# New prices and transfer rules in the planner that orders a fused feed-forward kernel

## The chip, the cores and the metric

The kernel runs on one core of a Trainium2 chip. Each core has a matrix engine (TensorE, PE in the profile), a vector engine (VectorE, DVE), a scalar engine (ScalarE, ACT), a general engine (GpSimd, POOL) and SyncE (SP), which only issues transfers. Each engine works through its own list of instructions in order; they wait for one another by semaphores. Transfers are issued by an engine's queue and carried out by 16 DMA engines. The metric is the time on the device in microseconds (us).

## The reference

Inputs are x (4 batches x 1024 tokens x 512), a condition (4 x 128) and three weights: norm_w (512 x 128), up_w (4096 x 512) and down_w (512 x 2048). In float32:

```python
scale = cond @ norm_w.T + 1.0
ms = jnp.mean(x * x, axis=-1, keepdims=True)
h = x * (scale[:, None, :] * jax.lax.rsqrt(ms + EPS))
u = h @ up_w.T
val, gate = jnp.split(u, 2, axis=-1)
h = val * jax.nn.gelu(gate, approximate=False)
hq = act_quant(h)      # 8 bits, a scale for each token
wq = weight_quant(down_w)   # -1, 0 or 1, one scale: the mean of |down_w|
return hq @ wq.T + x
```

## The kernel before

**What is computed where.** The up-projection is done with 16-bit floats in high and low parts, so that one product of float32 matrices becomes six matmuls. The first of the four batches is multiplied plainly, in 16 pieces of weights by two halves of 512 tokens (`plain_half`, products by L897, the product of the two halves of the projection by VectorE at L925). While it runs, the weights of each piece are prepared for the later batches: loaded from DRAM (`w_load`, L581), their largest magnitude taken (`w_largest`, L589) and from it a power of two and gain factors (L467, L595 to L604), turned on TensorE (`w_turn`, L625), split into high and low (L639 to L661), summed for a scheme of fast matrix multiplication (L673 to L689), and spilled to a DRAM scratch (`s_spill`, L693). The down weights are loaded (L740), summed (L744) to the mean (L753 to L755) and rounded (L759, L760). Batches two to four use the fast scheme: seven products of half size for each pair of pieces (`product`, L882; copies and combinations L960 to L999), with weight forms reloaded from scratch. The rows of h are then quantised (L1011 to L1086) and multiplied by the down weights in 8-bit floats (L1102, L1153), scaled and added to x (L1111, L1193), and stored.

**The condition.** The scale of each channel is worked out early on VectorE (`scT`, L510, L514) in a layout with channels on partitions. Batches 1 to 3 need it in rows instead: `cond_rows` (L551) writes each column of `scT` to `rows_dram`, 128 x 4 values of four bytes at scattered places, one transfer for each batch, `cond_load_scale` (L556) reads one back, repeated on all partitions, into `sc` (256 KB), and `cond_bring` (L560, VectorE) scales it, for the tokens of the next batch (L829).

```python
SP.dma_start(out=rows_dram[b].rearrange("(k p) -> p k", p=P), in_=scT[:, :, b])   # L551
SP.dma_start(out=sc, in_=rows_dram[b].partition_broadcast(P))                     # L556
DVE.tensor_scalar(sc, sc, ux[:, b : b + 1], None, ALU.mult)                       # L560
```

**The planner.** No engine is called directly. The kernel's functions run against recorders, which note every instruction as a step: its engine, the steps it depends on (by what it reads and overwrites) and its price. `Plan.order` then orders the steps, and `emit` issues them in that order, which is the order of every engine's list. Semaphores are derived from the dependencies afterwards, so that the result of any order is right. The first 150 steps (HEAD) of each engine keep their recorded order. The rest is found in 40 rounds:

- `needed` works out for every step the latest time at which it may start without delaying TensorE, from the times of the round before.
- `place` takes the steps by that latest time and gives each the first free stretch on its engine's line behind its dependencies, with a margin of up to 0, 0.3, 0.6 or 0.9 us, changing from round to round.
- `replay` runs the order through a model of the engines, and sets the prices and times for the next round. Then six replays with chance (each cost but TensorE's times 0.95 to 1.09, each of SyncE's transfers up to 1 us later) give a mean end, and the order with the least mean is taken.

`price` gives for each step its time alone, its time beside work on the port which VectorE and GpSimd share, and for a transfer the time that it keeps the DMA engines. A transfer counts 1.2 us from issue to start and 1.5 us from its last byte to landing. SyncE's transfers share one line, "DMA", one behind the other; ScalarE's don't stand on it. ScalarE issues three transfers: one load in the head, `cond_load_rest` (L488, which brings the condition of batches 1 to 3) and the last store.

Of the kernel before, what the change touches and what calls it, by code (L numbers as in the profile page):

```python
# [78 lines left out]
def _free(v):  # L79
    n = 1  # L80
    for d in v.shape[1:]:
        n *= d
    return n
# [28 lines left out]
class Plan:  # L112
# [12 lines left out]
    def add(self, eng, method, real, args, kwargs):  # L125
# [6 lines left out]
        writes = [a for w, a in operands if w]  # L132
        reads = [a for w, a in operands if not w]
        s.alone, s.beside, s.wait = price(eng, method, writes, reads, args, kwargs)
        deps = set()
        for v in reads:
# [36 lines left out]
        if not s.wait:  # L173
            if s.n < HEAD and eng in self.last:
                deps.add(self.last[eng])
# [5 lines left out]
    def order(self):  # L181

        steps = self.steps
        for s in steps:
            s.after, s.cost = [], (s.alone + s.beside) / 2
        for s in steps:
            for d in s.deps:
                steps[d].after.append(s)
        clock = 0.0
        for s in steps:  # L190
            if s.eng == "PE":
                s.start = clock
                clock += s.cost
        best, chance = None, random.Random(1)
        for n in range(ROUNDS):
            self.needed(clock)
            self.place(0.3 * (n % 4))
            order = sorted(steps, key=lambda s: (s.start, s.n))
            clock = self.replay(order)
            late = sum(self.replay(order, chance) for _ in range(MISSES)) / MISSES  # L200
            if best is None or late < best[0]:
                best = late, order
            self.replay(order)
        self.replay(best[1])
        return best[1]
# [5 lines left out]
            for t in s.after:  # L211
                s.late = min(s.late, t.late - lag(s, t) - s.wait - s.cost)

    def place(self, margin):

        steps = self.steps
        used = {e: Line() for e in ("PE", "ACT", "DVE", "POOL", "SP", "DMA")}
        for s in sorted(steps, key=lambda s: (s.late, s.n)):  # L220
            t = max((steps[d].end + lag(steps[d], s) for d in s.deps), default=0.0)
            if s.eng != "PE":
                t += min(margin, max(0.0, s.late - t) * 0.1)
            if s.wait and s.eng == "SP":
                t = used["DMA"].put(t + ISSUE, s.wait) - ISSUE
            s.start = used[s.eng].put(t - s.before, s.before + s.cost) + s.before
            s.end = s.start + (ISSUE + s.wait + LANDING if s.wait else s.cost)

    def replay(self, order, chance=None):

        steps = self.steps
        free = dict.fromkeys(("PE", "ACT", "DVE", "POOL", "SP", "DMA"), 0.0)
        port = {"DVE": 0.0, "POOL": 0.0}
        for s in order:
            e = s.eng
            t = free[e] + s.before
            for d in s.deps:
                t = max(t, steps[d].end + lag(steps[d], s))
            cost = s.alone
            if s.beside > s.alone:  # L240
                x = port["POOL" if e == "DVE" else "DVE"] - t
                if x > 0:
                    cost += (s.beside - s.alone) * min(1.0, x / s.alone)
                port[e] = t + cost
            if chance:
                cost *= 1.0 if e == "PE" else 0.95 + 0.14 * chance.random()
            else:
                s.cost = (s.cost + cost) / 2 if e in port else cost
            s.start, s.end = t, t + cost
            free[e] = s.end  # L250
            if s.wait and e != "SP":
                s.end = t + ISSUE + s.wait + LANDING
            elif s.wait:
                free["DMA"] = max(free["DMA"], t + ISSUE) + s.wait
                s.end = free["DMA"] + LANDING + (chance.random() if chance else 0.0)
        return max(s.end for s in order)
# [6 lines left out]


HEAD = 150
ROUNDS, MISSES, ISSUE, LANDING, RELOAD = 40, 6, 1.2, 1.5, 6.5


class Line:
# [2 lines left out]
    def __init__(self):  # L272
        self.spans = []

    def put(self, t, cost):
        v = self.spans
        n = bisect.bisect_right(v, (t, 1e9))
        if n and v[n - 1][1] > t:
            t = v[n - 1][1]
        while n < len(v) and v[n][0] < t + cost:  # L280
            t = v[n][1]
            n += 1
        v.insert(n, (t, t + cost))
        return t


def lag(s, t):

    if s.eng == t.eng:
        return 0.0  # L290
    if s.eng == "PE":
        return 0.2
    return 0.08 if t.eng == "POOL" else 0.05


def price(eng, method, writes, reads, args, kwargs):

    out = writes[0]
    n = _free(out)
    if "dma" in method:  # L300
        nbytes = n * out.shape[0] * mybir.dt.size(out.dtype)
        if "transpose" in method:
            return 0.45 + nbytes / 32768 * 0.16, 0.0, nbytes / 32768 * 0.17
        last = min(v.ap[-1][1] * mybir.dt.size(v.dtype) if v.ap[-1][0] == 1 else 4 for v in (out, reads[0]))
        return 0.45, 0.0, nbytes / (290e3 if last >= 1024 else 1.5e3 if last < 64 else 150e3)
    wide = max([n] + [_free(v) for v in reads if len(v.shape) > 1])
    psum = any(str(v.space).endswith("PSUM") for v in reads)
    if eng == "PE":
        f32 = any(v.dtype == F32 for v in reads)
        return (max(n, 64) * (2 if f32 else 1) / 2.4 + 2.5) / 1e3, 0.0, 0.0  # L310
    if eng == "ACT":
        cost = 0.08 + wide * 0.0009 + (0.05 if method != "copy" else 0) + (0.05 if psum else 0)
        return cost, 0.0, 0.0
    if eng == "POOL":
        if method == "partition_all_reduce":
            return (1.8 if wide > 1 else 0.4), 0.0, 0.0
        if method == "tensor_scalar":
            cost = 0.2 + wide * 0.00092
            return cost, cost * 1.2, 0.0
        cost = 0.75 if wide <= 8 else 0.18 + wide * 0.00195  # L320
        return cost, cost * 1.42, 0.0
    if method == "reciprocal":
        return 0.17 + max(0, wide - 8) * 0.0056, 0.0, 0.0
    if wide <= 32:
        return 0.17, 0.0 if psum else 0.44, 0.0
    if psum or method in ("tensor_reduce", "memset"):
        return 0.1 + wide * 0.00108, 0.0, 0.0
    if method == "tensor_scalar":
        cost = 0.1 + wide * 0.00052
        return cost, cost * 2.2, 0.0  # L330
    if method == "tensor_tensor" and all(v.dtype in (BF16, F16) for v in reads):
        cost = 0.1 + wide * 0.00052
        return cost, cost * 1.6, 0.0
    cost = 0.1 + wide * 0.00106
    return cost, cost * (1.35 if method == "scalar_tensor_tensor" else 1.8), 0.0


class Rings:
# [30 lines left out]
def glu_quant_kernel(  # L369
# [557 lines left out]
    def plain_first(between):  # L927

        ps = {1: bank("B", 1, name="pg_0_0"), 0: bank("A", 2, name="pv_0_0")}
        gate, a21, a22 = a_parts(0)  # L930
        order = [(1, w, 0, k) for w in range(2) for k in range(2)]
        order += [(1, w, 0, k) for k in range(2, NK) for w in range(2)]
        order += [(0, w, 0, k) for w in range(2) for k in range(NK)]
        order += [(t, 0, 1, k) for t in (1, 0) for k in range(NK)]
        for n, (t, w, l, k) in enumerate(order):
            if n in between:
                between[n]()
            a = [gate[:, 0], gate[:, 1]] if t else [a21, a22]
            a = a[k // 2].rearrange("p w (k f) -> p w k f", k=2)
            PE.matmul(  # L940
                ps[t], a[:, w, k % 2, :], XP[:, l, k, :TOK],
                start=w + l + k == 0, stop=l == 1 and k == NK - 1,
            )
        t1 = wpool.tile([P, TOK], F32, name="g_0_0", tag="t1")
        ACT.activation(t1, ps[1], AF.Gelu, scale=gain(0, 1))
        DVE.scalar_tensor_tensor(h_half(0, 0), ps[0], gain(0, 0), t1, ALU.mult, ALU.mult)
# [167 lines left out]
    class Pair:  # L1114
# [12 lines left out]
        def sum1(self, place):  # L1127
            self.s[1] = place.bitcast(BF16)
            DVE.tensor_tensor(self.s[1], self.part(1, 0), self.part(1, 1), ALU.add)
# [759 lines left out]
```

## Time and profile before

| | us |
|---|---|
| median of 3 timed runs | 742.27 (742.14 to 743.57) |
| the profiled execution, its own time | 737.92 |
| its span, first to last instruction | 736.1 |

The granted clock of TensorE was 0.998 in the profiled execution. How the page's other numbers are read: an engine's busy time is the time in which it ran instructions that are counted; the rest of the span it waited, or issued. A group or a timeline row gives the line of the kernel, the operation, what it writes and reads, and the shape; x4 means four alike in a row. Of a matmul of 512 columns the duration shown (0.38 us) is longer than the distance between two of them in a row, since they are pipelined. For transfers the row on SPq is only the issue; the time to landing is given apart.

The page's shares by engine in 40 slices show where TensorE is not at 90% or more of the time:

```profile
## 2 busy tenths in 40 slices
PE   6999999999999999999999999999999999999998
DVE  5976899999888767989878988798768888865997
ACT  4876646676245775535344577743333666333373
POOL 1465887789214000714002300750001000000000
DMA  8788678999954444695943445697753444443414
```

Each digit is a slice of 18.4 us. Only the first and the last slices stand under 9. The DMA engines are busiest in slices 4 to 12, which is the first batch, in which weights are loaded and spilled.

### The profile page before, as it was taken

The page shows a single profiled execution, that of the slowest core. Times are in us where ns is not written, and L with a number is a line of the kernel's source. Part 1 is how long each engine was busy: PE and PEld are TensorE (multiplying, and loading weights), DVE is VectorE, ACT ScalarE, POOL GpSimd, SP SyncE. Part 2 cuts the span into 40 slices and gives each one's busy share as a digit, 9 for nine tenths or more (in the row PEclk, how much of TensorE's full clock was granted, in tenths as well). Part 3 has the DMA queues.
Part 4 walks back from the last instruction along what each step waited for, and adds up shares of the span by engine and source line. Part 5 has one row for each costly group of instructions (what it writes and reads, how often), then busy time and mean ns, then how long its engine had stood idle before and what let it go on. Part 6 is the DMA issues. An engine that isn't in the chain of part 4 may idle for free.

```text
span 736.1 us, 10201 instructions
## 1 busy us (share of the span) xinstructions
PE 723.8 (98%) x3684; PEld 363.2 (49%) x3684; DVE 606.6 (82%) x833; ACT 392.1 (53%) x635; POOL 215.5 (29%) x213
## 2 busy tenths in 40 slices
PE   6999999999999999999999999999999999999998
PEld 3554444444444445655444445656444444444754
DVE  5976899999888767989878988798768888865997
ACT  4876646676245775535344577743333666333373
POOL 1465887789214000714002300750001000000000
PEclk9999999999999999999999999999999999999999
DMA  8788678999954444695943445697753444443414
GB/s 267 244 175 206 192 203 210 233 250 236 229 162 101 100 102 137 159 206 154 233 135 101 108 101 140 159 208 155 183 141 106 97 100 108 104 101 97 144 38 164
DMA packets 179567, 115.74 MB, mean 157 GB/s; under 512 B 141750, under 2 KB 147767, under 8 KB 179516
## 3 DMA queue, kind: packets, MB, share of 16 engines
q1 hardware_dynamic: 179226, 114.76, 60.7%
q10 hardware_dynamic: 290, 0.33, 0.3%
q8 instruction: 29, 0.48, 0.3%
q14 instruction: 22, 0.18, 0.1%
HBM read 58.93 MB, written 23.09 MB: 111 GB/s over the span
## 4 chain that ended last, share of the span: by engine, by line
PE 88%; DMA 5%; DVE 3%; ACT 3%; issue 1%; POOL 1%; SPq 0%; POOLq 0%; DVEq 0%
PE A L882 33%; PE E L882 17%; PE B L882 8%; PE po L1153 8%; PE E L897 8%; PE B L897 4%; PE A L897 4%; DMA rows_dram<-scT 2%; PE po L1102 2%; PE E L1102 1%; PE A L1102 1%; DMA s_dram<-R 1%; DMA H<-in_x_dram 1%; DMA am<-in_x_dram 1%; ACT R L1218 1%
## 5 line engine op out<-in xcount | busy, mean ns | idle before, releaser
L882 PEld LDWEIGHTS <-SXY 128*128 128x128 f16 x2016 | 197.2, 98 | 229.8 <-issue 2.1
L882 PE MATMUL A<-R,SXY 128*128 128x512 f16 x1152 | 270.5, 379 | 0.3 <-ACT t L960 0.3
L882 PE MATMUL E<-R,SXY 128*128 128x512 f16 x576 | 142.9, 379 | 0.0
L1032 POOL PARTITION_ALL_REDUCE am<-R x8 | 17.3, 2158 | 249.1 <-DVE R L1018 249.1
L1074 DVE TENSOR_TENSOR H<-H,am 128x1024 f32<-128x1024 f32 x64 | 78.7, 1260 | 0.1
L897 PEld LDWEIGHTS <-SXY 128*128 128x128 f16 x462 | 45.1, 98 | 53.5
L882 PE MATMUL B<-R,SXY 128*128 128x512 f16 x288 | 70.8, 379 | 0.0
L1016 DVE TENSOR_REDUCE gm<-H 128x512 f32<-128x1024 f32 x56 | 68.9, 1230 | 0.7
L980 DVE SCALAR_TENSOR_TENSOR H<-A,sg,t 128x512 f32<-128x512 f32 x48 | 35.9, 748 | 36.0 <-PE A L882 35.7
L968 ACT COPY B<-A 128x512 f32<-128x512 f32 x48 | 27.4, 570 | 60.1 <-PE A L882 56.7
L1153 PE MATMUL po<-wd,R 128*128 128x256 fp8e4 (+1 forms) x448 | 59.0, 275 | 0.0
L993 ACT ACTIVATE t<-t,sg 128x512 f32<-128x512 f32 x48 | 34.7, 722 | 39.2 <-DVE t L990 39.1
L1153 PEld LDWEIGHTS <-R 128*128 128x128 bf16 (+1 forms) x480 | 47.0, 98 | 15.9
L960 ACT COPY t<-A 128x512 f32<-128x512 f32 x48 | 28.1, 586 | 48.9 <-PE A L882 48.8
L990 DVE TENSOR_TENSOR t<-E,t 128x512 f32<-128x512 f32 x48 | 33.0, 688 | 24.4 <-PE E L882 24.0
L977 ACT ACTIVATE t<-B,sg 128x512 f32<-128x512 f32 x48 | 33.0, 687 | 34.5 <-PE B L882 34.0
L786 POOL TENSOR_SCALAR ssq<-ssq 128x2 f32<-128x2 f32 x12 | 5.5, 456 | 155.4 <-ACT H L816 114.1
L897 PE MATMUL E<-R,SXY 128*128 128x512 f16 x210 | 49.6, 379 | 0.0
L996 DVE TENSOR_TENSOR v<-A,v 128x512 f32<-128x512 f32 x48 | 33.1, 689 | 19.7 <-PE A L882 18.0
L972 ACT COPY v<-E 128x512 f32<-128x512 f32 x48 | 28.1, 586 | 34.0 <-PE E L882 31.6
L1018 DVE TENSOR_TENSOR R<-R,gm 128x512 f32<-128x512 f32 x56 | 44.4, 792 | 0.8
L897 PEld LDWEIGHTS <-R 128*128 128x128 f16 x282 | 27.5, 98 | 33.6 <-issue 1.3
(232 smaller groups left out, 1082.0 us busy)
## 6 DMA issues: line engine op xcount, KB each, us to landing
SXY<-s_dram SPq DMA_DIRECT2D x66, 256.0 KB, 2.7
SXY<-s_dram SPq DMA_DIRECT2D x18, 384.0 KB, 3.6
H<-in_L_cond_up_w_dram SPq DMA_DIRECT2D x13, 512.0 KB, 4.9
s_dram<-SXY SPq DMA_DIRECT2D x14, 384.0 KB, 4.9
xr<-in_x_dram SPq DMA_DIRECT2D x19, 256.0 KB, 3.3
out_dram<-xr SPq DMA_DIRECT2D x19, 256.0 KB, 3.6
H<-in_x_dram SPq DMA_DIRECT2D x8, 512.0 KB, 5.5
R<-in_L_cond_down_w_dram SPq DMA_DIRECT2D x8, 512.0 KB, 6.5
```

The costliest lines, as they stand in the source:

```text
L882: PE.matmul(o, s[:, w, k, :], tv[:, :, c, l, k, :], start=start and n == 0, stop=stop and n == len(TERMS) - 1, skip_group_check=True,)
L897: PE.matmul(ps, a[k // 2][:, w, k % 2, :], XP[:, l, k, h * TOK : (h + 1) * TOK], start=n == 0, stop=n == len(terms) - 1,)
L977: ACT.activation(cur["t1"], pb, AF.Gelu, scale=gain(g, 1))
L980: DVE.scalar_tensor_tensor(h_half(g - 1, 0), prev["A"], gain(g - 1, 0), prev["t1"], ALU.mult, ALU.mult)
L990: DVE.tensor_tensor(prev["t2"], prev["E"], prev["t2"], ALU.add)
L993: ACT.activation(prev["t2"], prev["t2"], AF.Gelu, scale=gain(g - 1, 1))
L996: DVE.tensor_tensor(cur["v"], cur["A"], cur["v"], ALU.add)
L1016: DVE.tensor_reduce(gm[0], v, AX.X, ALU.max, apply_absolute_value=True)
L1018: return [largest, lambda: DVE.tensor_tensor(m, m, gm[0], ALU.max)]
L1074: DVE.tensor_tensor(v, v, r.to_broadcast([P, 2, TOK]), ALU.mult)
L1102: PE.matmul(po.rearrange("p (y c o) -> p y c o", c=2, o=P), q[:, a, h, j], wd8[:, :, j // n, j % n, :, y0:y1].rearrange("p c o y -> p y c o"),
L1153: PE.matmul(po, w[:, j], m, start=start and j == 0, stop=stop and j == n - 1, skip_group_check=True,)
```

## The change

Nothing of the kernel itself is touched, only the planner that orders it.

- `place` counts the stretch on the DMA line for every transfer that lasts more than 0.1 us, of any engine (before: every transfer of SyncE, none of ScalarE). In `replay` likewise: transfers of up to 0.1 us are off the DMA line, all others are on it, with chance.
- `place` gets a second number beside the margin, a guard: a step of an engine other than TensorE that would stand within 1 us of its latest time takes up to that much of free time ahead of it, which no later step may use. The four pairs of margin and guard take the place of the four margins.
- The replays with chance vary costs by 0.96 to 1.08, and lengthen each step that uses the shared port by up to 0.6 of the difference between its price beside other work and alone.
- Prices change on ScalarE (a copy of 512 from 0.54 to 0.53, other work of 512 to 0.7, or 0.62 out of the accumulators), GpSimd (the price beside other work, from 1.42 to 1.2 times for wide operations) and VectorE (a few per cent, and the factors beside other work).

```diff
-            self.place(0.3 * (n % 4))
+            self.place(*MARGINS[n % len(MARGINS)])
...
-            if s.wait and s.eng == "SP":
+            if s.wait > 0.1:
                 t = used["DMA"].put(t + ISSUE, s.wait) - ISSUE
-            s.start = used[s.eng].put(t - s.before, s.before + s.cost) + s.before
+            near = 0.0 if s.eng == "PE" or s.late - t > 1.0 else guard
+            s.start = used[s.eng].put(t - s.before, s.before + s.cost, near) + s.before
...
             if chance:
-                cost *= 1.0 if e == "PE" else 0.95 + 0.14 * chance.random()
+                cost *= 1.0 if e == "PE" else 0.96 + 0.12 * chance.random()
+                if s.beside > s.alone:
+                    cost += 0.6 * (s.beside - s.alone) * chance.random()
...
-            if s.wait and e != "SP":
+            if 0.0 < s.wait <= 0.1:
                 s.end = t + ISSUE + s.wait + LANDING
...
+MARGINS = ((0.3, 0.0), (0.3, 0.15), (0.3, 0.3), (0.25, 0.1))
...
-    def put(self, t, cost):
+    def put(self, t, cost, guard=0.0):
...
-        v.insert(n, (t, t + cost))
+        free = v[n - 1][1] if n else 0.0
+        v.insert(n, (max(free, t - guard), t + cost))
...
-        cost = 0.08 + wide * 0.0009 + (0.05 if method != "copy" else 0) + (0.05 if psum else 0)
+        cost = 0.12 + wide * 0.0008 + (0.05 if psum else 0)
+        if wide == 512 and method != "copy":
+            cost = 0.62 if psum else 0.7
...
-        return cost, cost * 1.42, 0.0
+        return cost, cost * (1.2 if wide > 256 else 1.42), 0.0
...
-        return 0.1 + wide * 0.00108, 0.0, 0.0
+        return 0.1 + wide * (0.00116 if wide == 512 else 0.00105), 0.0, 0.0
...
-        cost = 0.1 + wide * 0.00052
-        return cost, cost * 2.2, 0.0
+        cost = 0.08 + wide * 0.00051
+        return cost, cost * 1.85, 0.0
...
-    cost = 0.1 + wide * 0.00106
-    return cost, cost * (1.35 if method == "scalar_tensor_tensor" else 1.8), 0.0
+    cost = 0.1 + wide * 0.00101
+    more = 1.45 if wide > 512 or method == "scalar_tensor_tensor" else 1.8
+    return cost, cost * more, 0.0
```

More of the change, by code (lines that the diff above doesn't have):

```diff
@@ L212, in needed, with place @@
                 s.late = min(s.late, t.late - lag(s, t) - s.wait - s.cost)
-    def place(self, margin):
+    def place(self, margin, guard):
         steps = self.steps
```

## The prediction

> **What bounds the kernel now.** I read the page's head and busy times first, then the list of TensorE's waits, and for each of them the timelines and the chain of waits around it. The page:
>
> ```profile
> span 736.1 us, 10201 instructions
> PE 723.8 (98%) x3684; PEld 363.2 (49%) x3684; DVE 606.6 (82%) x833; ACT 392.1 (53%) x635; POOL 215.5 (29%) x213
> ```
>
> TensorE is busy for 723.8 of 736.1 us, so at most 12.3 us can be won by any other order of the same instructions, and the change alters nothing but the order. TensorE has three waits of more than 0.2 us behind the head. In the timeline (start, duration, engine and line, shapes, in brackets the idle time before and who ended it) they stand so, with the work that they waited for:
>
> ```profile
> 65.89 1.03 PE L897 MATMUL E<-R 128*128 128x512 f16 x4
> 66.75 0.60 PE L625 MATMUL po<-ident,H 128*128 128x128 f32 x4
> 74.53 1.03 PE L897 MATMUL E<-R 128*128 128x512 f16 x4
> 77.12 1.03 PE L897 MATMUL E<-R 128*128 128x512 f16 x4
> 79.19 1.02 PE L897 MATMUL E<-R 128*128 128x512 f16 x4 [1.05 <-DVE H L925]
> 80.06 0.28 PE L753 MATMUL po<-wpart,one 128*128 128x1 f32 x2
> ...
> 222.82 0.72 ACT L824 ACTIVATE xn<-xn,rs 128x512 f32<-128x512 f32 x1 [2.41 <-POOL rs L787]
> 224.63 0.57 ACT L960 COPY t<-A 128x512 f32<-128x512 f32 x1
> 225.25 2.75 PE L882 MATMUL A<-R,SXY 128*128 128x512 f16 x12 [0.29 <-ACT t L960]
> ...
> 492.76 1.74 DVE L865 TENSOR_TENSOR H<-H 128x1024 f16<-128x1024 f32 x1
> 493.98 0.38 PE L882 MATMUL A<-R,SXY 128*128 128x512 f16 x1
> 494.42 0.86 DVE L1193 SCALAR_TENSOR_TENSOR xr<-po,dq,xr 128x256 f32<-128x256 f32 x2
> 495.34 0.27 PE L1153 MATMUL po<-wd,H 128*128 128x256 fp8e4 x1 [0.98 <-DVE xr L1193]
> ```
>
> From row 65.89 to row 66.75, four 512-wide products issue in 0.86 us, 0.215 each. By that pace the four at 77.12 are out at 77.98 and the next stands until 79.19: **1.21 us lost**. The single product at 493.98 is out at 494.20, the next at 495.34: **1.14 lost**. The third I put at **0.45**: by the pace of 0.215 the products before it are out at 224.8, the next starts at 225.25. These 2.8 us are what a better order can win behind the head; the head's first 150 instructions keep their recorded order, so its waits stay.
>
> The 1.21 has a long history. The chain of waits, from 41 us on:
>
> ```profile
> 41.38 12.25 DMA rows_dram<-scT
> 54.08 6.37 DMA am<-in_x_dram
> 64.65 7.88 DMA s_dram<-R
> ...
> 75.10 1.14 DVE wam L589
> 76.25 1.43 DVE wam L467
> 78.40 0.75 DVE H L925
> ```
>
> One slow transfer, `rows_dram` (2 KB in four-byte pieces), holds SyncE, which waits for it before it can issue its reader `sc`; then a spill, a copy, a maximum and the product of two halves follow each other up to TensorE. SyncE's own timeline, its wait, and the issue-to-landing times of L551 and of L556:
>
> ```profile
> 41.38 0.97 SPq L551 DMA_DIRECT2D rows_dram<-scT  x2
> 47.25 0.35 SPq L693 DMA_DIRECT2D s_dram<-SXY  x1
> 53.70 0.33 SPq L556 DMA_DIRECT2D sc<-rows_dram  x1
> 56.17 0.37 SPq L581 DMA_DIRECT2D H<-in_L_cond_up_w_dram  x1
> 64.65 0.36 SPq L693 DMA_DIRECT2D s_dram<-R  x1
> 68.47 0.37 SPq L581 DMA_DIRECT2D H<-in_L_cond_up_w_dram  x1
> ...
> SPq L556 <- DMA rows_dram<-scT: 5.6, 1, 5.6
> ...
> DMA to landing us min/median/max: 12.1/12.1/12.1
> ...
> DMA to landing us min/median/max: 4.3/4.3/4.3
> ```
>
> **The change, part by part.** Prices, guards and chance alter only where the planner puts steps. Every step, with its dependencies, is in both programs, so nothing is added or removed: TensorE moves 236 of 3680 steps at the least, VectorE 295 of 827, ScalarE 177 of 598, GpSimd 43 of 209, SyncE 82 of 360. Most moves swap neighbours of one price far from a deadline. I looked for those that touch the waits above, or that stand closer to TensorE than before.
>
> *1. The first `rows_dram` transfer moves behind a weight load.* Before, SyncE issues both at 41.38. In the changed order the weight load issued at 56.17 (L581) stands ahead of it, and that load waits until TensorE has turned the weights whose place it takes. TensorE's order there:
>
> ```profile
> 50.14 0.60 PE L625 MATMUL po<-ident,H 128*128 128x128 f32 x4
> 55.54 0.60 PE L625 MATMUL po<-ident,H 128*128 128x128 f32 x4
> ```
>
> The turn at 55.54 is moved to four products behind the one at 50.14: four turns (50.14 to 50.58, 0.44) and four products (0.86) put it at 51.44, its results at about 52.0. The load issues then (0.37), and `rows_dram` at about 52.4: **11 us later than before**. At 12.1 us to landing it is there at 64.5; `sc` is issued then and lands 4.3 later, at **68.8**. Queued behind SyncE's wait: the spill of L693 (before at 64.65, now at 64.8), the other two `rows_dram` transfers, and the weight load that was issued at 68.47.
>
> *2. Its user moves ahead on VectorE, and a product with slack loses it.* Rows of VectorE:
>
> ```profile
> 66.87 0.74 DVE L925 SCALAR_TENSOR_TENSOR H<-E,sg,t 128x512 f32<-128x512 f32 x1
> 67.53 0.47 DVE L560 TENSOR_SCALAR sc<-sc,ux 128x512 f32<-128x512 f32 x1
> 73.16 0.69 DVE L658 TENSOR_TENSOR R<-po,R 128x512 f16<-128x512 f32 x1 [2.26 <-ACT R L649]
> 75.02 1.21 DVE L589 TENSOR_REDUCE wam<-H 128x2 f32<-128x1024 f32 x1
> 79.06 1.21 DVE L640 TENSOR_TENSOR H<-H 128x1024 f16<-128x1024 f32 x1
> ```
>
> Before, the L925 at 66.87 ran first and the product that needs it came at 74.53: 6.9 us of slack. Now L560, which waits for `sc`, stands ahead of that L925, and TensorE's product is moved up: behind the four at 65.89 come the two small L753 products (before at 80.06; 0.22 for both) and then this one, at 66.98. It can start at 68.8 + 0.47 + 0.74 + 0.06 = 70.1: **a new wait of 3.1 us**. The wait begins to exist if `sc` lands after 65.7.
>
> *3. What becomes of the 1.21.* The spill now issues at 64.8; at 7.88 the copy of L649 and L658 follow at 73.3 on, as before. Between L658 and the L925 that TensorE waits for stand now L661 (0.42), L640 and L760 (1.21 each), an L925 (0.74), L759 (1.21), L589 (1.21), L467 (0.17 to 1.43) and L595 (0.17). With L658's 0.69 and the last 0.74 that is 7.8 to 9.0, less 0.07 of overlap at each of nine joints: 7.1 to 8.4, so it ends at 80.4 to 81.7. TensorE, 3.1 late, wants it at 77.98 + 3.1 = 81.1. Its product starts at 81.1 to 81.7 instead of 79.19: **+1.9 to +2.5**. The L589 among them also needs the weight load of 68.47, which landed for it by 75.02, 6.5 us later. It is now issued behind the turn of its predecessor's weights, late by the new wait (71.5), and behind the two other four-byte transfers (65.2). At 6.5 it lands at 78.0, just before VectorE comes to L589 (about 78.2). But before, a copy waited for the spill issued at 47.25 behind two such transfers:
>
> ```profile
> 57.73 0.59 ACT L649 CAST SXY<-po 128x512 f16<-128x512 f32 x1 [3.42 <-DMA s_dram<-SXY]
> ```
>
> That is 4.1 after `rows_dram` landed (53.63), though issued 10.5 earlier. If the load too lands 4.1 after the two (65.2 + 12.2 + 4.1 = 81.5), then L589, L467, L595 and L925 (2.1 with the overlaps) end at 83.6: +4.5. The other bound: if `rows_dram` lands as fast as `sc` (4.3), `sc` is there at 61 and the spill is issued four to seven us earlier; then nothing waits, and the 1.21 goes: −1.2. I take **+2.8** out of −1.2 to +4.5, near the values that only repeat measured landings, with a little of B's below.
>
> The Trainium skill's page "DMA: Bandwidth & Descriptors", section "Anatomy of one DMA — SWDGE (gpsimd) path", gives some 2 us of fixed cost for a transfer, nearly all of it the receipt of the write; by that `rows_dram` would land at an estimated 54.5 and step 2 would cost nothing. The trace's 12.1 us speaks against it. The same page, "Queues, rings and completion order", says that a transfer's semaphore write lands only after every earlier write of its SDMA engine; that fits 12.1 us for 2 KB, and would hold the transfers behind the four-byte ones as well.
>
> *4. The 0.45 at 225.* The two L824 scalings that waited for GpSimd stand elsewhere; L960's copy follows an L1082 whose input is there. **−0.45**; at worst 0.
>
> *5. The 1.14 at 494.* VectorE does the 1.74 us of L865 ten steps earlier, and comes to the two L1193 (0.86 for both) straight from L999; a reduction and a maximum of 1.91 in all move up too and take back most of that. TensorE has two other products of L882 (0.43) before this one, so wants it at 494.63 at the earliest; the L1193 end at about 494.6. **−1.14** at best. Some new short wait among the several hundred moved steps, with TensorE at 98%, is to be expected; I know its price only by the waits listed (0.3 to 1.0), and put one of 0.5 against these two. Together −1.1, bounds −1.6 and 0.
>
> *6. The tail.*
>
> ```profile
> 730.04 0.75 DVE L1111 SCALAR_TENSOR_TENSOR R<-A,dq,R 128x512 f32<-128x512 f32 x1 [1.21 <-PE A L1102]
> ```
>
> Near 720 an output step L1111 goes ahead of an L1074, which delays it by 0.74; VectorE's idle 1.21 before 730.04 covers that. Without the cover it is 0.74. I take **+0.2**.
>
> Sum: 2.8 − 1.1 + 0.2 = +1.9 on 736.1, a span of 738.0. The profiled execution took 737.92 us in all, 1.8 around the span, and the median of the runs shown is 742.27, 4.35 above it. With both kept: 739.8 for a profiled execution and **744.2 for the median**.
>
> **The rivals.**
>
> *A. `rows_dram` lands quickly (faster).* At 41.38 two went out together, behind the spill of 36.87; alone it may be quick. As long as `sc` lands within 13.3 us of the issue of `rows_dram` (52.4 to 65.7), nothing waits. Then −1.2 − 1.1 = −2.3: 740.0, down to 739.5 if no new wait comes. For it: half the small pieces. Against it: its pieces remain four bytes long, and the load issued just ahead is one of the largest, 512 KB.
>
> *B. The two later four-byte transfers hold the weight load (slower still).* It decides when that load lands after 78.2. Then +4.5 − 1.1 + 0.2 = +3.6: 745.9; with a further wait of a microsecond at the weights after it, 747. For it: the spill of 47.25. Against it: the load is issued 6 us behind the small transfers, when half their time is over.
>
> *C. It cancels.* A landing in between, `sc` at 67.0: the new wait is 1.3, TensorE wants the later product at 79.3, VectorE has it at 78.6 to 79.9, so +0.1 to +0.7; with −1.1 and +0.2 that is −0.8 to −0.2, 741.8 in the middle. For it: 12.1 us is the figure of a pair, and half a pair may take some of it.
>
> **How the numbers follow.** Forecast 0.37, B 0.20, C 0.19, A 0.24. This kernel's measurement can't tell less than 0.2% (1.5 us) from no change. Slower is the forecast and B, with a little of the forecast's low side given to same: 0.55; same 0.21; faster 0.24. The range takes A's 740.0 and B's with its further wait, 739.7 to 747.3; the likeliest one's own is 743.2 to 745.5.
>
> **What would show it.** Right: SyncE issues `rows_dram` near 52 and `sc` near 64; TensorE waits about 3 us for an L925 at 67; no wait at 225 and 494; the span 1.5 to 3 us longer. Step 1 is wrong if `sc` is issued within 8 us of `rows_dram`; step 3 if TensorE's wait near 78 to 81 exceeds 0.6 beyond the first; and the whole if a wait over 1 us stands behind 90 us, where I saw none.

## The result: 0.9% slower, and where the time went

The changed kernel took 747.72 us (median of 6, 744.90 to 749.56), the kernel before 741.69 (6 runs, 738.21 to 743.57); the ratio is 1.0088, 95% interval 1.0063 to 1.0114. Run again beside the experiments on another chip it was 1.0112 (1.0085 to 1.0140). Forecast was +1.9 us with a range up to 747.3; the loss is 6 to 8 us. One execution of the experiments, the profiled one of the first, took 1095 us at a granted clock of 0.656; the ratios leave it out, and its profile is not read here. The head and the busy times of the page after:

```profile
span 743.1 us, 10203 instructions
PE 726.9 (98%) x3684; PEld 362.5 (49%) x3684; DVE 608.0 (82%) x833; ACT 390.6 (53%) x635; POOL 211.2 (28%) x213
```

The span of the profiled execution grew by 7.0 us. TensorE's work is the same but for 3.1 us more of busy time, of which 2.5 are a matter of its clock (below). From the list of TensorE's waits of the changed kernel (for whom; total, times, longest):

```profile
PE E L906 <- DVE H L934: 6.8, 3, 3.0
```

Lines of the changed kernel are 9 higher than before: L934 is the product of two halves that was L925. Where there was one wait of 1.0 for it, there are three with 6.8. TensorE's timeline of the changed kernel, where they are, and two later ones:

```profile
62.39 1.03 PE L906 MATMUL E<-R 128*128 128x512 f16 x4
65.54 1.02 PE L906 MATMUL E<-R 128*128 128x512 f16 x4 [2.01 <-DVE H L934]
67.79 0.33 PE L634 MATMUL po<-ident,H 128*128 128x128 f32 x1 [0.46 <-ACT R L660]
78.48 1.02 PE L906 MATMUL E<-R 128*128 128x512 f16 x4 [1.73 <-DVE H L934]
82.55 1.86 PE L906 MATMUL E<-R 128*128 128x512 f16 x4 [3.04 <-DVE H L934]
88.48 1.89 PE L906 MATMUL E<-R 128*128 128x512 f16 x8
...
314.06 0.81 PE L891 MATMUL A<-R,SXY 128*128 128x512 f16 x3 [0.35 <-ACT t L969]
...
412.81 1.46 PE L891 MATMUL A<-R,SXY 128*128 128x512 f16 x6 [0.87 <-DVE H L989]
...
733.89 0.60 PE L1111 MATMUL A<-wd,R 128*128 128x512 fp8e4 x2 [0.23 <-ACT R L1095]
```

The same products stand in the timeline of before at other times, so the loss can be read off as a shift. The four products at 62.39 are those of 65.89 before: **3.5 us earlier**, a gain of the head that the forecast didn't have. Those at 82.55 are those of 79.19: 3.35 later, so 6.85 were lost in between. The eight at 88.48 stood before at 82.78, by this row of TensorE's timeline before:

```profile
82.78 1.89 PE L897 MATMUL E<-R 128*128 128x512 f16 x8
```

That is 5.7 later: 2.35 more were lost while TensorE had work. From there the shift stays at 5.7 to 225 us, and then changes by −0.18 (225), +0.51 (314), +0.92 (412, where before had 0.11), −1.14 (494) and +0.41 (734); the last store takes 0.76 longer to land. Sum: −3.5 + 9.2 − 0.18 + 0.51 + 0.92 − 1.14 + 0.41 + 0.76 = +7.0.

Nearly all of the loss is in the 9.2 us between 63 and 88 us. Its chain of waits in the changed kernel, and SyncE's timeline there:

```profile
49.04 10.09 DMA rows_dram<-scT
59.20 5.12 DMA sc<-rows_dram
...
68.15 12.04 DMA H<-in_L_cond_up_w_dram
...
81.74 0.76 DVE H L934
```

```profile
49.04 0.46 SPq L560 DMA_DIRECT2D rows_dram<-scT  x1
...
59.64 0.37 SPq L702 DMA_DIRECT2D s_dram<-R  x1
60.06 1.47 SPq L560 DMA_DIRECT2D rows_dram<-scT  x2
...
68.15 0.37 SPq L590 DMA_DIRECT2D H<-in_L_cond_up_w_dram  x1
```

The first transfer of four-byte pieces lands 10.1 us after its issue, and TensorE waits at 65.54 for what stands behind `sc`. The two others go out at 60.06. The weight load issued at 68.15 then takes 12.0 us, and TensorE waits for its maximum until 82.55. What the DMA engines do in this time shows in the view by stretches (the last number of a row is GB/s, the one before the share of time in which the DMA engines are busy, the third from the end TensorE's granted clock):

```profile
49.00:53.00 4.00, 4.00 (x20) 1.83 (x19) 2.88 (x8) 4.00 (x10) 1.59 (x3) 1.00 0.99 255
53.00:62.00 9.00, 9.00 (x44) 4.06 (x43) 6.18 (x14) 6.25 (x12) 8.54 (x11) 1.00 0.45 15
...
67.00:76.00 9.00, 8.54 (x43) 3.92 (x41) 2.96 (x5) 3.72 (x7) 0.68 (x1) 1.00 0.74 37
76.00:80.00 4.00, 1.78 (x8) 0.62 (x7) 3.53 (x3) 3.80 (x7) 3.92 (x4) 1.00 0.70 229
```

Twice, for nine us each, the engines move 15 and 37 GB/s in place of some 250, though transfers have been issued: in the first pause the read of `sc` and a spill, from 59.2 on, in the second the weight load of 68.15. Each pause begins four to seven us after a group of `rows_dram` transfers was issued. The kernel before had such a pause as well, behind its first two `rows_dram` transfers, and behind the third, after the spill of 64.65, a shorter and weaker one; TensorE was busy through both:

```profile
42.00:46.00 4.00, 4.00 (x22) 2.12 (x21) 3.46 (x11) 3.34 (x6) 3.33 (x6) 1.00 0.93 305
46.00:53.00 7.00, 7.00 (x38) 3.73 (x37) 4.69 (x11) 5.85 (x13) 4.43 (x6) 1.00 0.78 56
...
65.00:70.00 5.00, 5.00 (x29) 2.80 (x27) 4.65 (x11) 4.35 (x9) 4.55 (x6) 1.00 0.96 120
```

### The profile page after: what moved, and what is told of

Read it like the earlier page. It is cut to its first block, busy times and chain, and to the rows that moved or that the text cites. A ratio compares the mean times of both kernels' runs of the same rounds, so it can differ in the third digit from the quotient of the medians.

```text
span 743.1 us, 10203 instructions
## 1 busy us (share of the span) xinstructions
PE 726.9 (98%) x3684; PEld 362.5 (49%) x3684; DVE 608.0 (82%) x833; ACT 390.6 (53%) x635; POOL 211.2 (28%) x213
## 4 chain that ended last, share of the span: by engine, by line
PE 86%; DVE 6%; DMA 4%; ACT 1%; POOL 1%; issue 1%; SPq 0%; DVEq 0%; ACTq 0%
PE A L891 32%; PE E L891 16%; PE E L906 9%; PE B L891 8%; PE po L1162 8%; PE A L906 5%; PE B L906 4%; DVE H L1083 2%; DMA H<-in_L_cond_up_w_dram 2%; DMA rows_dram<-scT 1%; DMA H<-in_x_dram 1%; DMA sc<-rows_dram 1%; PE A L1111 1%; PE po L634 1%; DVE H L1008 1%
## 5 line engine op out<-in xcount | busy, mean ns | idle before, releaser
L1041 POOL PARTITION_ALL_REDUCE am<-R x8 | 15.4, 1922 | 286.3 <-DVE R L1027 286.3
L906 PE MATMUL E<-R 128*128 128x512 f16 x162 | 39.9, 385 | 6.8 <-DVE H L934 6.8
L1091 ACT ACTIVATE H<-H 128x1024 f32<-128x1024 f32 x38 | 40.2, 1057 | 10.2 <-DVE H L1083 10.2
L1027 DVE TENSOR_TENSOR R<-R,gm 128x512 f32<-128x512 f32 x56 | 40.7, 728 | 0.9
```

What stands on the lines that cost most here:

```text
L906: PE.matmul(ps, a[k // 2][:, w, k % 2, :], XP[:, l, k, h * TOK : (h + 1) * TOK], start=n == 0, stop=n == len(terms) - 1,)
L1027: return [largest, lambda: DVE.tensor_tensor(m, m, gm[0], ALU.max)]
L1091: ACT.activation(v, v, AF.Copy, bias=MAGIC)
```

## The experiments

Most kernels take the order that a planner made and move single steps in it: `moved` puts, on its engine's list, the first step of each pair ahead of the second, and merges the lists again so that each step follows those it depends on; everything else stays. The change to the code is alike in each:

```diff
-        return best[1]
+        return moved(best[1])
```

So only the pairs are given below. Step 114 is `cond_load_rest`; 521, 522 and 523 are the three `rows_dram` transfers, 677 the read of `sc`, 757 `cond_bring`. Ratios are to the kernel before on the same chip, with the 95% interval.

### The load of the condition and the head

The order of before, with the load out of the head:

```diff
+MOVES = ((114, 379),)
```

> The order of before, with one step moved: ScalarE's load of the condition of batches 1 to 3 (cond_load_rest, 192 KB repeated on all partitions) is issued where the changed kernel has it, behind the copies near 25 us, and no longer at 1.4 us. Theory H (this load slows the transfers of the head, and TensorE's wait of 3.6 us at 12 us is its price): the wait at 12 us shrinks to about 0.5 and the time falls by 2.5 to 3.5 us. Rival C (the head of the two profiled executions differed by chance): no change within 0.7 us.

Measured: 735.75 against 737.32, 1.6 us less by the medians, 2.1 by the ratio of 0.9972 (0.9959 to 0.9985). The other way round, the changed kernel with the load back in the head:

```diff
+MOVES = ((114, 46),)
```

> The order of the changed kernel, with the same load put back to 1.4 us. Theory H: 2.5 to 3.5 us longer than the changed kernel, so about 9 to 10 us longer than before, with TensorE waiting again over 3 us at 12 us. Rival C: as the changed kernel, 6 to 6.5 us longer than before.

Measured: ratio 1.0127 (1.0113 to 1.0141), some 1 to 3 us over the changed kernel (1.0088, 1.0112); against the second of these the difference is not clear of the noise. The cause shows in the stretch from 2 to 6 us, first in the kernel before, then in this one, then in the changed kernel:

```profile
2.00:6.00 4.00, 4.00 (x12) 1.33 (x10) 2.97 (x21) 0.78 (x2) 0.00 (x0) 1.00 0.95 188
```

```profile
2.00:6.00 4.00, 4.00 (x11) 1.35 (x10) 2.94 (x21) 0.77 (x2) 0.00 (x0) 1.00 0.91 162
```

```profile
2.00:6.00 4.00, 4.00 (x11) 1.34 (x10) 2.86 (x21) 1.24 (x3) 0.00 (x0) 1.00 0.97 307
```

With the load in the head the DMA engines are as busy and move little more than half as much: 162 to 188 GB/s against 307. ScalarE gets the first tokens accordingly, in before and in the changed kernel:

```profile
8.08 0.63 ACT L1218 ACTIVATE R<-H 128x512 f32<-128x512 f32 x1 [5.29 <-DMA H<-in_x_dram]
```

```profile
5.53 0.63 ACT L1227 ACTIVATE R<-H 128x512 f32<-128x512 f32 x1 [2.75 <-DMA H<-in_x_dram]
```

Theory H holds in sign. Its size was too high: TensorE's wait at 12 us is 3.3 to 3.7 in the three profiles with the load in the head, and anywhere from 0.5 to 3.2 in those without it. The first profile of the changed kernel had the best of these; by the two runs the move is worth some 1 to 2 us on the average.

### The place of the four-byte transfers

SyncE's list of before, in the changed kernel:

```diff
+MOVES = ((581, 577), (521, 577), (522, 577), (358, 577), (408, 577), (677, 577),
+         (758, 577), (482, 577), (523, 577), (426, 577), (580, 577), (479, 577))
```

> The order of the changed kernel, with twelve transfers of SyncE between 41 and 78 us put back into the order of before (two rows_dram transfers ahead of the weight loads, the third behind the read of sc); VectorE's and TensorE's order stay changed. Theory R (the place of the rows_dram transfers makes TensorE's waits of 65 to 88 us, 9 us with the half clock): these waits go but for about 1 us, and the time is 2.5 to 3.5 us below before, 8 to 9.5 below the changed kernel. Rival V (VectorE's new order, L569 ahead of the L934 that TensorE needs, makes them): 2 us below the changed kernel at most, still 4 us over before.

Measured: ratio 1.0108 (1.0094 to 1.0122), nothing won. `sc` was read at 56.13, three us earlier than in the changed kernel, and the waits at 78 and 82 are gone, but another has come, by VectorE's and TensorE's timelines of this run:

```profile
58.23 0.42 DVE L695 TENSOR_TENSOR SXY<-po,SXY 128x256 f16<-128x256 f32 x1 [6.02 <-ACT SXY L686]
...
69.24 0.74 DVE L959 SCALAR_TENSOR_TENSOR H<-E,sg,t 128x512 f32<-128x512 f32 x1
```

```profile
70.03 1.86 PE L931 MATMUL E<-R 128*128 128x512 f16 x4 [3.83 <-DVE H L959]
```

(Lines here are 25 higher than in the changed kernel.) VectorE stood for 6.0 us until 58.23, because a spill issued behind the first pair of `rows_dram` transfers was held, worked without rest from 60 to 70, and came to the product that TensorE wants at 66 (L959) at 69.24. TensorE's granted clock fell within this wait and was at half until 74.8. The time is what V expected, but the wait comes from the held spill and not from the place of `cond_bring`. Neither theory as it stood: in the new order of TensorE and VectorE, a pause 10 us earlier costs as much as one in its new place.

Only the second and third transfers away, to 158.6 us:

```diff
+MOVES = ((522, 1242), (523, 1242))
```

> The order of the changed kernel, with only the second and third rows_dram transfers moved, from 60 us to about 166 us. Theory R2 (a burst of four-byte writes keeps the 16 DMA engines from other work for some 8 us, and the burst of 65 us held the spill of 59.6 and the weight load of 68.2): the wait for sc at 63.4 us stays (2.2 us), the weight load lands within 7 us, the waits at 78 and 82 us and the half clock behind them go: 6 to 7.5 us below the changed kernel, at or a little below before. Rival T (the load was late because it was issued behind TensorE's late turn, and the spill because it was queued behind SyncE's wait): 1.5 us below the changed kernel at most. A new wait of some us near 166 us would speak for R2 as well.

Measured: ratio 1.0111 (1.0095 to 1.0126). The waits at 78 and 82 and the half clock are gone as R2 expects, and the gain is lost again where the transfers went. TensorE's timeline of this run, and the transposing transfer behind them on SyncE:

```profile
64.99 1.02 PE L931 MATMUL E<-R 128*128 128x512 f16 x4 [1.21 <-DVE H L959]
...
183.58 4.44 PE L931 MATMUL B<-R,SXY 128*128 128x512 f16 x12 [3.53 <-ACT t L955]
198.51 1.24 PE L916 MATMUL E<-R,SXY 128*128 128x512 f16 x5 [1.44 <-DVE H L959]
```

```profile
161.73 10.99 SPq L902 DMA_TRANSPOSE R<-nx  x1
```

There the mere issue of the next transfer took 11.0 us. The time is the one T expected, but its reason falls: the weight load, issued at 67.60 as late as in the changed kernel (68.15), landed after 4.9 us and not 12.0, so it was late because of the two transfers, not because of TensorE's late turn. Behind the wait at 183 the clock was at half again, for 3.5 us. The wait at 198 is new: one of 1.0 stands at 199.7 in the run before this too; the profile of the changed kernel, where TensorE comes later, has none there.

### VectorE's order, and one group of transfers

`cond_bring` directly ahead of its first reader, nothing else:

```diff
+MOVES = ((757, 807),)
```

> The order of the changed kernel, with one step of VectorE moved: cond_bring (L569), which waits for sc, stands no longer ahead of the product of two halves (L934) that TensorE needs, but directly ahead of the first step that reads sc (L838). Theory R2 (the burst of four-byte writes at 65 us sets when the spill and the weight load behind it land, and so TensorE's last wait): the wait of 2.15 us at 63.4 goes, but the wait behind the weight load grows by most of it; 0 to 1 us below the changed kernel. Rival V (each wait counts for itself): 2.2 us below the changed kernel.

Measured: ratio 1.0118 (1.0098 to 1.0139), nothing won. The wait at 65 is gone, and those behind the weight load are 3.4 and 2.1:

```profile
79.34 1.85 PE L931 MATMUL E<-R 128*128 128x512 f16 x4 [3.42 <-DVE H L959]
83.28 1.86 PE L931 MATMUL E<-R 128*128 128x512 f16 x4 [2.08 <-DVE H L959]
```

V falls: these waits are not added one by one; the landing of the weight load (issued at 67.32, 13.5 us) sets the last of them, and what is spared in front is waited behind. Now the same with all three transfers issued together at 50 us:

```diff
+MOVES = ((522, 758), (523, 758), (757, 807))
```

> As the run before (cond_bring late), and the second and third rows_dram transfers issued directly behind the first (49 us), so that there is one burst of four-byte writes and none at 65 us. Theory R2: one pause of the DMA engines behind 51 us, none behind 65; the spill and the weight load land in 7 us or less; TensorE has no wait over 0.7 us between 40 and 100 us and no half clock; 7 to 9 us below the changed kernel, so 0.5 to 2.5 below before. Rival N (the pause grows with the number of four-byte pieces): the first pause is three times as long, some 25 us, and the time is above the changed kernel's.

Measured: 740.58 against 737.01, ratio 1.0051 (1.0034 to 1.0068). Its stretches, and TensorE's waits of over half a microsecond from 40 to 200 us:

```profile
53.00:62.00 9.00, 9.00 (x43) 4.13 (x42) 7.16 (x15) 6.28 (x13) 7.79 (x10) 1.00 0.55 29
62.00:70.00 8.00, 7.54 (x41) 4.02 (x39) 3.88 (x8) 3.77 (x8) 3.73 (x5) 1.00 0.87 336
```

```profile
77.12 1.02 PE L931 MATMUL E<-R 128*128 128x512 f16 x4 [0.60 <-DVE H L959]
192.87 1.24 PE L916 MATMUL E<-R,SXY 128*128 128x512 f16 x5 [1.20 <-DVE H L959]
```

One pause, not two, and it is as long with three transfers (1536 pieces) as with one (512): N falls. In the stage it does what R2 says: the weight load, issued at 67.05, lands after 5.0 us. It gains 3 to 5 us and not 7 to 9. The later waits of the new order now count, 1.2 us at 193 and 0.8 at 201, which the profile of the changed kernel does not have, and the wait at 12 us is 2.6 here.

The same on the order of before:

```diff
+MOVES = ((114, 379), (523, 358))
```

> The order of before, with the load of the condition behind the copies near 25 us as in the first run, and the third rows_dram transfer issued with the other two at 41 us, not at 57. Theory R2: no pause behind 62 us, so the spill of L693 at 65 us lands in 5 us and no longer in 7.9, and TensorE's wait of 1.21 us at 78 goes: 1 us below the first run, 3 below before. Rival N (the pause grows with the pieces): the first pause is half as long again (12 us), sc is read 4 us later than before, and the time is no lower than the first run's.

Measured: 735.52 against 737.01, ratio 0.9975 (0.9963 to 0.9987). In its profile TensorE does not wait between 40 and 220 us by more than about 0.2 at a time, and the wait of 1.21 is gone. In the times that last microsecond can't be told from the first run's 0.9972, and the 3 us below before that R2 expected were not reached.

### Without four-byte pieces

```diff
-        for b in range(1, B):
-            SP.dma_start(out=rows_dram[b].rearrange("(k p) -> p k", p=P), in_=scT[:, :, b])
+        n = (B - 1) * NK
+        cols = sm.tile([P, B - 1, NK], F32, name="cols", bufs=1)
+        DVE.tensor_copy(cols, scT[:, :, 1:].rearrange("p k b -> p b k"))
+        pr = po_bank("prow", [n, P])
+        PE.transpose(pr, cols.rearrange("p b k -> p (b k)"), ident)
+        row = sm.tile([n, P], F32, name="row", bufs=1)
+        DVE.tensor_copy(row, pr)
+        SP.dma_start(out=rows_dram[1:].rearrange("b (k p) -> (b k) p", p=P), in_=row)
```

> The changed planner, and cond_rows without four-byte pieces: the twelve columns of scT are put in order (VectorE), turned by TensorE into 12 rows of 128, copied (VectorE) and written in one transfer of 12 pieces of 512 bytes; four small instructions and one transfer in place of three transfers. The planner orders anew. Theory R2: no pause of the DMA engines, the transfer lands in 3 us, no wait of TensorE over 1 us between 40 and 100 us: 7 to 9 us below the changed kernel. Rival P (the reading of the weights and the spills at 60 to 80 us are too much for the DMA engines, whatever the pieces): waits of 3 us or more remain there, 3 us below the changed kernel at most.

Measured: 737.98 against 737.01, ratio 1.0013 (0.9997 to 1.0029): 5.5 to 7 us below the changed kernel, and as fast as before. The transfer is issued at 69.11, and behind it the engines go on:

```profile
72.00:80.00 8.00, 8.00 (x40) 3.82 (x38) 6.29 (x11) 5.98 (x11) 5.98 (x7) 1.00 1.01 249
```

TensorE has no wait of 0.3 us or more between 40 and 220 us. P falls: the load and the spills of this stage are not too much for the DMA engines. This run also plans anew, so it doesn't prove by itself that the pieces make the pause; with the fourth run, in which the pause went where the transfers went, it leaves little else.

### The change's parts

The changed kernel beside the next three runs:

> The changed kernel as it is, on the chip of the other runs of this call. By all theories 0.7 to 1.1% longer than before; its head shows how much of the wait at 12 us is chance: theory H (with the load of the condition out of the head that wait is short) has 0.5 to 1 us there as in its first profile, rival C anything up to 3.5.

Measured: 744.76 against 737.11, ratio 1.0112 (1.0085 to 1.0140). Its wait at 12 us is 1.9, neither theory's end: the load moved, and chance is left.

The planner of before with the new rule for transfers alone:

```diff
-            if s.wait and s.eng == "SP":
+            if s.wait > 0.1:
...
-            if s.wait and e != "SP":
+            if 0.0 < s.wait <= 0.1:
```

> The planner of before with one part of the change, the rule for transfers (those over 0.1 us on the DMA line, of any engine). TensorE's, VectorE's and GpSimd's orders come out as before; the load of the condition leaves the head, and of SyncE's transfers one for x, the second rows_dram transfer (now behind the read of sc) and two weight loads move by a place or two. Theory S (the loss comes from the new orders of TensorE and VectorE, which leave no slack for the pauses; the rule itself gains by the head): 1.5 to 2.5 us below before. Rival M (the rule makes the loss): 3 us or more over before.

Measured: 742.35 against 737.11, ratio 1.0055 (1.0027 to 1.0083), with single times from 735.4 to 745.4. One row of TensorE's timeline:

```profile
80.62 1.86 PE L897 MATMUL E<-R 128*128 128x512 f16 x4 [3.01 <-DVE H L925]
```

The other way round, the changed planner with that rule undone (the same four lines, reversed):

> The changed planner with that one part undone: new prices, guards and chance, the old rule for transfers. The load of the condition is back in the head, TensorE's and VectorE's orders are nearly those of the changed kernel. Theory S: the waits of 65 to 88 us stay, and the head's wait is as before: 1 to 3 us over the changed kernel. Rival M: 3 us or more below the changed kernel.

Measured: 747.28, ratio 1.0132 (1.0109 to 1.0155). The load of the condition is back in the head, and the weight load issued at 69.52 lands after 11.75 us:

```profile
81.29 1.22 DVE L598 TENSOR_REDUCE wam<-H 128x2 f32<-128x1024 f32 x1 [5.90 <-DMA H<-in_L_cond_up_w_dram]
```

Neither theory alone. The rule loses by itself, since it splits the pair of transfers at 41 us into one at 40.4 and a second at 52.1, near the third (56.2), and the spill of 63.23 lands after 10.7 us where it took 7.9. The new prices, guards and chance lose by themselves too, and more. Why single times of the run with the rule alone lie 10 us apart stays open.

### Both kernels beaten

The run with one group on the order of before, and two further moves: the two L824 (2025, 2027) behind the copy of L960, and L865 (4131) behind the two L1193.

```diff
+MOVES = ((114, 379), (523, 358), (2027, 1776), (2025, 1776), (4131, 3486))
```

> The run with one burst on the order of before, and two more repairs: ScalarE's two token scalings (L824, which wait for GpSimd at 222 us) behind the copy that TensorE waits for (L960), and VectorE's L865 of 492.8 us behind the two results (L1193) that TensorE waits for. Each wait counts for itself: the waits of 0.45 at 225 and 1.14 at 494 go, 1.6 us below the run with one burst, 0.45 to 0.5% below before. Rival W (a step that is moved out of the way makes a wait behind it): new waits of 0.5 to 1 us near 227 or 500, and no gain over that run.

Measured: 732.84 against 737.11, ratio 0.9940 (0.9921 to 0.9960). Its page's span, and the first row of the list of TensorE's waits:

```profile
span 730.7 us, 10200 instructions
```

```profile
PE po L1267 <- DVE wam L492: 2.0, 1, 2.0
```

It is in the head, as are the others of the list. W falls: the two moves made no wait behind them, and none of the waits that the profile of before had behind 40 us is left. It is 0.6% below before and 1.5 to 1.7% below the changed kernel.

## Why the prediction was wrong

**The head: a step that was not in the sum.** The prediction said that "the head's first 150 instructions keep their recorded order, so its waits stay". They do not for transfers: the planner ties a step to the one before it on its engine only `if not s.wait`, and a transfer has a wait. (Its test `s.n < HEAD` also counts the steps of the whole program, not 150 for each engine.) Step 114, the load of the condition, left the head, and the head became 1 to 2 us shorter (3.5 in the profile). The row of the load's issue at 1.4 us was there; what it did to the other transfers was costed at nothing. That the median came out only 0.4 us above the range is luck: this gain hid part of a loss that was sized far too small.

**Step 1 was right.** `rows_dram` went out at 49.04 and `sc` landed at 64.3; forecast were 52.4 and 68.8, and 3.5 of the difference are the head. It landed 10.1 us after its issue (12.1 in the trace of before); the 2 us that follow from the Trainium skill's page "DMA: Bandwidth & Descriptors", section "Anatomy of one DMA — SWDGE (gpsimd) path", are not what these transfers take in any run here; that section fits its figure to transfers that GpSimd issues, and these are SyncE's.

**Step 2 was right in mechanism, 2.15 us in place of 3.1.** But it is not a loss of its own: taken away, nothing was won (1.0118).

**Step 3 is where the prediction failed.** It took +2.8 of a range up to +4.5, and 9.2 came. Its term for the weight load repeated a landing of 6.5 us, measured before on a load that was issued 11.9 us behind the last four-byte transfer; 8.1 us behind two of them it was 12.0, by the mechanism of rival B, and 10.7 to 13.5 in the four other runs that keep two of them ahead of that load (the order of the changed kernel, or nearly). With the two moved away it was 4.9 and 5.0. The trace of before already had the right row: the load of 47.70, issued 6 us behind the pair of 41.38, landed after 11.7 us, which answers what the prediction held against B. B's own bound of +4.5 still was too small for three reasons. It held only the load as late, while the spill issued just ahead was held as well, from 59.64 until ScalarE's copy at 72.65 (forecast 7.9 us, measured 13.0). ScalarE's row:

```profile
72.65 0.58 ACT L658 CAST R<-po 128x512 f16<-128x512 f32 x1 [4.92 <-DMA s_dram<-R]
```

It counted a single last wait, while TensorE has two products there, at 78.48 and 82.55, each with a wait of its own. And it had nothing for the clock. In the view by stretches, the granted clock of the changed kernel:

```profile
76.00:82.00 6.00, 1.78 (x8) 0.62 (x7) 5.25 (x7) 4.29 (x8) 5.40 (x6) 0.90 0.84 219
82.00:88.00 6.00, 5.45 (x14) 1.92 (x14) 6.00 (x7) 2.83 (x5) 4.58 (x3) 0.53 0.91 288
```

A mean of 0.90 over six us means half the clock for the last 1.2 of them, and one of 0.53 half the clock for the first 5.6: TensorE had half its clock from 80.8 to 87.6 us, and the sixteen products from 82.55 to 88.48 took 5.9 us, where 16 times 0.215 are 3.4. That is 2.5 us lost without any wait. The Trainium skill's page "TensorE: Matmul & The Clock Gate", section "Part 1: The HAM clock gate (the "warmup" mystery)", says that TensorE falls to half clock after an idle window of about 3.4 us; here the clock fell 1.4 us into the wait of 79.3 to 82.5, with 1.9 us of another wait a little ahead of it, so the trace agrees in kind but not in the length. Nor is it the sum of two waits: in the run with SyncE's list of before the clock fell 1.7 us into a single wait of 3.8 us, and in the run with the load back in the head it did not fall in a wait of 3.3 us at 12 us. No run here shows a length of wait at which it falls.

**Step 4** gave 0.18 in place of 0.45, **step 5** its 1.14 in full. The new waits set against them at 0.5 came to 1.4 (0.51, 0.92): the forecast had put them too low. Another near 193 to 200 shows in the runs with one group and with two late transfers, in which TensorE comes there earlier. **Step 6** gave a wait of 0.41, where it said 0.2; the last 0.76 are a store that landed later.

Rival A was wrong: alone the first transfer took 10.1 us, and `sc` came 15.3 after its issue, where A and C needed 13.3 or 14.6.

## What to carry to other kernels

A transfer of hundreds of tiny writes has a price that does not stand in its own row: look at what the DMA engines move in the ten microseconds behind it, group such transfers, and put them where nothing else is waited for, or turn the data on TensorE first. Before a wait is costed by the sum of what stands in front of it, ask which landing comes last; and where TensorE will wait for several us, count in the products that may run at half clock behind the wait (2.5 us here).

## What the runs showed of the hardware

A group of four-byte writes to DRAM (512 pieces for a transfer) was followed by 7 to 9 us in which the 16 DMA engines together moved 15 to 56 GB/s in place of 230 to 340, with no sign that it grows with the group's size (512, 1024 or 1536 pieces), in the stretches shown; only behind the third transfer of the kernel before, 512 pieces, was it weaker, with 120 GB/s over 5 us. The 12 pieces of 512 bytes had no such pause. One load of 192 KB that repeats 1.5 KB on all partitions lowered what the engines moved from 2 to 6 us (162 to 188 against 278 to 311 GB/s) while they showed as busy as without it. TensorE's clock halved for 6.8 us from 1.4 us into a wait of 3.2 us, 0.9 us behind one of 1.9, and in another run for as long from 1.7 us into a single wait of 3.8 us.
